# A decoder layer on one core: weighted values of two chunks at a time, sums built in place, a new order

## The chip, the cores and the metric

One core of a Trainium2 chip runs the whole layer. The metric is the device time of one execution in microseconds (us). The engines are PE (matrix multiplications), DVE (VectorE), ACT (ScalarE), POOL (GpSimd) and SP, whose queue issues nearly all transfers. The time before is 3048.16 us, the median of three runs (3047.43 to 3048.79).

## The reference

The inputs are x and a context, both 64 x 128 x 512 in float32. One layer does this, where `_layernorm` has no weights:

```python
x = _layernorm(x + _L0_attn_ref(x, Wqkv, q_norm_w, k_norm_w, Wo))   # 16 heads of 32; RMS norm of q and k, rotary, causal
x = _layernorm(x + _L0_xattn_ref(x, ctx, ctx))                      # 8 heads
x = _layernorm(x + _L0_ffn_ref(x, weight))                          # both sides quantized to fp8 in blocks of 128

# cross attention: channels and positions change roles; q, k, v are (b, 128, 512)
qh, kh, vh = q.reshape(b*8, 16, 512), k.reshape(b*8, 16, 512), v.reshape(b*8, 16, 512)
qk = einsum('bdm,bdn->bmn', qh, kh) / sqrt(16)      # 512 x 512 scores for each head
ret = einsum('bmn,bcn->bcm', softmax(qk), vh)
```

Cross attention is the largest part: for each of the 64 batches and 8 heads it takes a softmax over 512 x 512 scores with a sum over only 16 rows.

## The kernel before

The program goes over 64 batches of 128 rows of x. Three stages of different batches are at work at the same time, and a planner in the kernel writes their operations out in one fixed order for each engine.

**Self attention** (`self_attention`). x is transposed, multiplied by the three thirds of `wqkv` (`project`, L322), normalized and rotated (DVE L435, POOL L441), transposed again (L328) to `hT`. Scores come in two halves, each of eight small matmuls with 32 rows (L462, row tiles of the array). For each of four groups of heads follow the mask addition and the negated maximum on DVE (L472, L475), four exponentials on ACT (L480), the reciprocal (L483), a scaling on POOL (L484), a transpose and a copy to `pT`. `outs` (L497) multiplies by v in column tiles of the array, 32 columns each; `wo` (L322), the sum with x (L508) and a layer norm give `x1`.

**Cross attention.** Half a batch, four heads, is a step s. Its j-th part, with j from 0 to 7, is half of a chunk of 128 of the 512 positions: chunk c = j // 2, and two of the four heads. `split` writes q and k as three bfloat16 parts (ACT L515 and L517, POOL L516 and L518) to DRAM; `stack` reads them back with 96 rows (L550 to the tiles `ks` and `qs`, three of each). `maxima` multiplies the stacks (L569, two matmuls into the one buffer mx) and reduces (DVE L572); after eight of them the negated maxima are split in three (L579 to L582), transposed (L586) and sent as three more rows into `qs` (L589). `scores` multiplies again with 99 rows (L604, the one buffer sc), and one exponential on ACT (L607) makes half of a tile `e`. `values` (L618) multiplies a chunk of e by v in four column tiles, summed over four chunks in the one bank av, and is called for every second j:

```python
if j % 2:
    values(j // 8, j % 8 // 2, av)
```

`gather` copies av out and sends it to `ac` (values) and to DRAM (sums); `cross_norm` gets the reciprocals (L643) by way of DRAM into a tile of their own, rb (L645), multiplies (POOL L647), adds x1 (DVE L649) and normalizes to x2.

**The last stage** (`ffn`). `quantize` (L370 to L388) scales x2 by blocks (POOL L374), rounds it to fp8's steps (DVE L377, L379, POOL L381, L382) and transposes it; four matmuls (L664), a scaled product each (DVE L669) into `ft`, a sum each into `h` (POOL L671), a layer norm and the transfer out. A layer norm is L353 to L360, with `rsqrt` (L341 to L347) inside; L347 is a product of 128 single numbers.

**Order.** `Plan.op` takes an engine, a cost in us, what is read and written, and a due time; `Plan.emit` places the operations one after another by these costs, hands out PSUM banks, and charges `TURN` where PE goes from one tiling (whole array, rows, columns) to another. The table `DUE` gives each operation of a batch its due time. The instructions are emitted in the order of placing, and each engine takes its own in that order. Four pools of banks exist: sc and mx with two banks each, av with one, t with three single ones, which everything else shares.

Of the kernel before, what the change touches and what calls it, by code (L numbers as in the profile page):

```python
# [38 lines left out]
    -0.477, 6.406, 1.108, 8.738, -3.388, -1.975, 8.446, -3.211, 10.046, 7.308, 7.14, 6.348, 8.835, 8.498,  # L39
    0.443, 6.255, 8.093, 0.86, -0.351, 5.636, 7.136, 7.206, 8.857, 1.225, 8.516, 5.911, -2.993, 7.459, 8.982,  # L40
    6.702, 8.584, -5.195, 1.613, 9.25, -1.205, 8.309, 8.351, 8.7, -4.37, 6.314, 5.681, -1.329, 2.961, 0.446,
    4.994, 7.225, 7.441, 9.169, -4.195, -1.969, 6.862, 8.415, 6.701, 5.583, 6.848, -2.311, 5.936, 0.669,
    -4.336, -3.225, -0.65, 7.359, 5.273, 5.221, 6.697, 1.056, -0.699, 10.521, 7.725, 1.786, 9.317, -0.281,
    7.711, 9.842, 9.061, 1.577, 8.221, 8.006, 7.879, 8.309, -3.567, 8.595, -1.665, 7.728, 9.366, -2.72, 8.659,
    7.918, 8.136, 1.226, 7.377, 8.801, -1.9, -3.235, 7.155, 2.459, 8.078, -0.111, 7.922, -2.283, 5.744, 8.589,
    8.639, 8.798, 8.023, 8.345, -2.381, 6.687, -3.336, 7.068, 9.022, 8.525, 7.703, -3.294, 7.204, 7.939,
    6.409, 8.724, 7.655, 6.335, -1.792, 9.28, 6.159, 8.745, 9.751, 6.105, 6.091, 9.536, -2.089, -2.232, 9.199,
    0.309, 6.288, 7.752, -2.402, 7.063, 8.465, 7.427, 8.775, 8.582, 6.962, 6.325, 8.669, -0.787, -1.292,
    0.453, 0.296, 8.463, 7.71, 7.588, 7.733, 0.379, 6.155, 7.154, 4.889, 7.773, -0.595, 7.767, 9.666, -1.092,
    6.191, 6.563, 6.653, 9.013, 8.943, 0.439, -2.316, 7.671, 0.863, 7.589, 6.814, 9.034, 7.913, 8.909, 0.355,  # L50
    6.804, 8.655, -2.295, 8.48, 8.501, 6.94, 8.017, 6.906, 7.026, 8.43, -1.393, 6.234, 7.098, 1.585, 8.045,
    8.533, 0.468, 7.066, 8.861, 0.714, 8.882, 6.175, -1.35, 6.235, 7.375, 6.217, 8.925, 8.641, -1.356, 0.11,
    7.185, 9.58, 7.556, -0.724, 6.008, 0.98, 6.563, 0.096, -0.199, 6.617, 4.512, 7.397, 6.433, 1.976, 0.624,
    8.166, 0.903, 8.672, 6.633, 8.659, 7.036, 7.95, 5.571, 1.956, 8.387, 7.208, 1.108, 8.445, 5.939, 7.611,
    9.168, 10.789, 9.282, 9.545, 7.415, 7.227, 1.509, 9.523, 0.675, 8.502, 1.884, 5.826, 8.269, 5.729, 9.384,
    0.745, 8.88, 8.088, 6.299, 9.017, 6.601, 5.232,
]
NK, NX, NE, NT = 3, 4, 2, 1
# [18 lines left out]
class Plan:  # L77
# [7 lines left out]
    TURN = 0.14  # L85
# [5 lines left out]
    def op(self, engine, cost, emit, r=(), w=(), b=None, due=0.0, late=0.0, mode=0):  # L91
# [24 lines left out]
        if b is not None:  # L116
            i = self.count[b] = self.count.get(b, -1) + 1
            due = b + (DUE[i] if i < len(DUE) else due)
        self.ops.append((engine, cost, emit, due, late, banks, sorted(deps), (b, i), mode))

    def emit(self):
# [14 lines left out]
        for _ in ops:  # L136
# [4 lines left out]
            for e in ENGINES:  # L141
                mine = None
                for n in cand[e]:
                    if at[n] > limit and e != "SP":
                        continue
                    t = max(est[n], free[e] + self.TURN * (e == "PE" and ops[n][8] != turned))
                    want = {}
                    for k in ops[n][5]:
                        if k.slot is None:
                            want[k.pool] = want.get(k.pool, 0) + 1  # L150
                    open_ = {p: sorted(s[1] for s in self.pools[p] if s[2] is None) for p in want}
                    if any(len(open_[p]) < m for p, m in want.items()):
# [35 lines left out]
def decoder_kernel(  # L188
# [24 lines left out]
    nc.sync.dma_start(out=cst, in_=consts)  # L213
# [11 lines left out]
    nc.scalar.copy(ident_h, ident)  # L225
# [11 lines left out]
    r_h = ring("h", 2, [P, D])  # L237
# [16 lines left out]
    r_rb = ring("rb", 1, [P, D])  # L254
# [3 lines left out]
    r_ft = ring("ft", 2, [P, D])  # L258
# [8 lines left out]

    banks = {
        "sc": [psp.tile([P, 2, D], F32, name="sc")],
        "mx": [psp.tile([P, 2, D], F32, name="mx")],  # L270
        "av": [psp.tile([P, D], F32, name="av")],
        "t": [psp.tile([P, D], F32, name=f"ps{i}") for i in range(3)],
    }

# [63 lines left out]
    def rsqrt(v, ky, s, col, pr):  # L338
# [4 lines left out]
        op("DVE", 0.07, lambda: nc.vector.scalar_tensor_tensor(t, r, v, r, ALU.mult, ALU.mult),  # L343
# [3 lines left out]
        op("DVE", 0.07, lambda: nc.vector.tensor_tensor(lv, r, t, ALU.mult), [ky + "r", ky + "t"], [ky + "l"], pr)  # L347
        return lv, ky + "l"

    def layernorm(h, kh, y, key, pr):  # L350
        s, k = small("ln")
        st, mv, ve = s[:, 0:6], s[:, 8:10], s[:, 10:11]
        op("DVE", 0.6, lambda: nc.vector.bn_stats(st, h), [kh], [k + "st"], pr)  # L353
# [4 lines left out]
        op("DVE", 0.08, lambda: nc.vector.scalar_tensor_tensor(nb, mv[:, 0:1], -1.0, r, ALU.mult, ALU.mult),  # L358
           [k + "mv", kr], [k + "nb"], pr)
        op("ACT", 0.5, lambda: nc.scalar.activation(y, h, AF.Identity, bias=nb, scale=r),  # L360
           [kh, k + "nb", kr], [key], pr)

    def quantize(src, key, pr):
# [4 lines left out]
        am, sc, rc = s[:, 0:NC], s[:, 8 : 8 + NC], s[:, 16 : 16 + NC]  # L368
        y, e, xq = r_qy[0], r_qe[0], r_xq[0]
# [4 lines left out]
        op("POOL", 0.97, lambda: nc.gpsimd.tensor_tensor(  # L374
# [6 lines left out]
        op("POOL", 1.2, lambda: nc.gpsimd.tensor_tensor(y, y, e, ALU.add), ["qy", "qe"], ["qy"], pr)  # L381
        op("POOL", 1.2, lambda: nc.gpsimd.tensor_tensor(xq, y, e, ALU.subtract), ["qy", "qe"], ["xq"], pr)  # L382
# [9 lines left out]
    def ffn_weights(o):  # L392

        wt, key = r_h[o % 2], f"h{o % 2}"
# [10 lines left out]
    def self_attention(b):  # L405
        at = lambda f: (b, f - 2.1)
        i2 = b % 2
        x_t, kx = r_x[i2], f"x{i2}"
        op("SP", 0.4, lambda: nc.sync.dma_start(out=x_t, in_=x[b]), [], [kx], at(-0.3), 5.0)
        xT, kxT = r_xT[i2], f"xT{i2}"  # L410
        tp = Bank("t", kxT)
# [3 lines left out]
        def project(j, pr, *then):  # L415
            ps = Bank("t", *then)
# [4 lines left out]
        for j in range(2):  # L421
# [7 lines left out]
            op("ACT", 0.7, lambda ps=ps, t1=t1, ss=ss: nc.scalar.activation(t1, ps.ap, AF.Square, accum_out=ss),  # L429
# [13 lines left out]
            tp = Bank("t", f"hT{j}{i2}")  # L443
# [10 lines left out]
        for r0 in (0, 2):  # L454
            pr = at(0.35 + 0.1 * r0)
            two = [Bank("t", f"pr{(4 * b + r0 + n) % 3}") for n in range(2)]
# [8 lines left out]
            for n in range(2):  # L465
# [16 lines left out]
                op("ACT", 1.55, exps, [k], [kp, k + "su"], pr)  # L482
# [3 lines left out]
                tp = Bank("t", f"{kpT}{r}")  # L486
# [3 lines left out]
        o_ps = Bank("t", "oT")  # L490
# [12 lines left out]
        a_ps = Bank("t", "h0")  # L503
        pr = at(0.87)
        matmuls(a_ps, pr, [(oT[:, c, :], wo[:, c, :]) for c in range(NC)], ["oT"])
        h, kh = r_h[0], "h0"
        pr = at(0.95)
        op("DVE", 0.6, lambda: nc.vector.tensor_tensor(h, a_ps.ap, x_t, ALU.add), [a_ps, kx], [kh], pr)  # L508
        layernorm(h, kh, r_x1[b % NX], f"x1{b % NX}", pr)

    def split(u, b, src, key, pr):
# [3 lines left out]
        op("ACT", 0.48, lambda: nc.scalar.copy(sp[:, 0, :], src), [key], [f"sp0{n}"], pr)  # L515
        op("POOL", 1.1, lambda: nc.gpsimd.tensor_tensor(rt, src, sp[:, 0, :], ALU.subtract), [key, f"sp0{n}"], [f"rt{n}"], pr)  # L516
        op("ACT", 0.48, lambda: nc.scalar.copy(sp[:, 1, :], rt), [f"rt{n}"], [f"sp1{n}"], pr)  # L517
# [39 lines left out]
    def maxima(j):  # L557
# [21 lines left out]
        op("DVE", 0.08, lambda: nc.vector.tensor_copy(ns[:, 0, :], x), kx, [f"ns{m}0"], pr)  # L579
# [30 lines left out]
    def values(s, c, av):  # L610
        b, g = divmod(s, 2)
        n = (4 * s + c) % NE
        e, va = r_e[n], r_va[b % 2]

        def go():
            for i in range(4):
                h = 4 * g + i
                nc.tensor.matmul(  # L618
                    av.ap[32 * i : 32 * i + 32, :], lhsT=va[:, c, 32 * h : 32 * h + 32], rhs=e[:, i, :],
                    start=(c == 0), stop=(c == NC - 1))  # L620
        op("PE", 0.83, go, [f"e{n}0", f"e{n}1", f"va{b % 2}"], [av], (b, g / 2 + (2 * c + 2) / 16), mode=COLS)
# [14 lines left out]
    def cross_norm(b):  # L636
        pr = (b, 1.15)
        n = b % 2
        x1, x2, ac, rs, rb = r_x1[b % NX], r_x2[b % 2], r_ac[n], r_rs[n], r_rb[0]
# [9 lines left out]
        op("DVE", 0.6, lambda: nc.vector.tensor_tensor(h, ac, x1, ALU.add),  # L649
           [f"ac{n}0", f"ac{n}1", f"x1{b % NX}"], [kh], pr)  # L650
        layernorm(h, kh, x2, f"x2{b % 2}", pr)

    def ffn(b):
        pr = (b, 1.35)
        x2, kx2 = r_x2[b % 2], f"x2{b % 2}"
        tp, half, sc, ks = quantize(x2, kx2, pr)
# [4 lines left out]
        h, kh = r_h[1], "h1"  # L661
        for c in range(NC):
            f_ps = Bank("t", f"ft{c % 2}")
# [4 lines left out]
            ft, kt = r_ft[c % 2], f"ft{c % 2}"  # L668
            op("DVE", 0.65, lambda f_ps=f_ps, ft=ft, c=c: nc.vector.scalar_tensor_tensor(  # L669
                ft, f_ps.ap, sc[:, c : c + 1], ws[:, c, :], ALU.mult, ALU.mult), [f_ps, ks, "ws"], [kt], pr)  # L670
            op("POOL", 1.2, lambda ft=ft, c=c: nc.gpsimd.tensor_tensor(h, h if c else x2, ft, ALU.add),  # L671
               [kt] if c else [kt, kx2], [kh], pr)
        pr = (b, 1.7)
        layernorm(h, kh, y, ky, pr)
# [13 lines left out]
    for j in range(-LEAD, 16 * B):  # L688
# [11 lines left out]
        if j % 2:  # L700
# [51 lines left out]
```

## Time and profile before

| | |
|---|---|
| median of 3 runs | 3048.16 us (3047.43 to 3048.79) |
| profiled execution | 3049.07 us, its span 3047.3 us |
| granted PE clock, mean | 0.983 |
| first scores (L604) start | 116.7 us |
| last scores start | 2999.1 us |
| from one batch to the next, steady | 45.14 us |
| mean of one L572 / L607 / L671 | 1221 / 1021 / 1269 ns |
| DMA, share of 16 engines | 27.6% for the queue that SP and the others issue to |

A window's row gives its length and each engine's busy time in it, then the granted clock (1.00 is full), the share of the DMA engines and GB/s. A timeline's row gives start, duration, engine, source line, operation, result and operands, their shapes and how many instructions were merged; a bracket holds the idle time before it and who ended it. PE's durations overlap those of the next instruction, so the cost of a step is read from one start to the next. A group's row ends with the sum and mean of its busy time and the idle time before it.

### The profile page before, as it was taken

What the parts mean: (1) busy time and instruction counts of PE and PEld (TensorE: products, weight loads), DVE (VectorE), ACT (ScalarE), POOL (GpSimd) and SP (SyncE); (2) the same over time, 40 slices, a digit from 0 to 9 for tenths busy, and PEclk for the clock granted to TensorE, in tenths of its full rate; (3) what the DMA queues carried; (4) which work ended last, traced back from release to release, by engine and by line L of the source; (5) the groups of instructions that cost most, each with busy time, mean ns of one, the idle gap of its engine ahead of it and who ended that gap; (6) DMA issues with size and microseconds to landing.
All of it is one profiled execution on the core that took longest, in us unless ns stands there. A gap on an engine that the chain in (4) does not pass through costs nothing.

```text
span 3047.3 us, 51833 instructions
## 1 busy us (share of the span) xinstructions
PE 2906.7 (95%) x17040; PEld 1307.0 (43%) x17040; DVE 2632.5 (86%) x5211; ACT 2296.3 (75%) x5382; POOL 1400.1 (46%) x1309
## 2 busy tenths in 40 slices
PE   7799999999999999999999999999999999999973
PEld 3334444444444444444444444444444444444420
DVE  3668899899899899889989989989989988988974
ACT  4467877777777787787787787777778778778763
POOL 3324444454445445444445445444444544444433
PEclk8899999999999999999999999999999999999996
DMA  3422322322222223232232232222222222223220
GB/s 114 61 83 79 89 80 82 89 82 84 84 84 85 83 83 85 85 86 81 82 89 81 80 89 82 83 86 84 84 82 87 83 85 86 81 82 89 75 65 25
DMA packets 162845, 249.97 MB, mean 82 GB/s; under 512 B 45328, under 2 KB 94608, under 8 KB 162448
## 3 DMA queue, kind: packets, MB, share of 16 engines
q1 hardware_dynamic: 161472, 242.47, 27.6%
q10 hardware_dynamic: 1104, 4.19, 0.4%
q8 instruction: 135, 2.21, 0.3%
q14 instruction: 134, 1.10, 0.1%
HBM read 159.01 MB, written 69.21 MB: 75 GB/s over the span
## 4 chain that ended last, share of the span: by engine, by line
PE 52%; DVE 26%; ACT 7%; issue 5%; DMA 5%; POOL 4%; SPq 1%; POOLq 0%; ACTq 0%; DVEq 0%
PE ps L322 17%; DVE nm L572 12%; PE mx L569 9%; PE av L618 8%; PE sc L604 8%; DVE ft L669 5%; PE ps L328 4%; DMA ks<-d_k 4%; POOL pr L484 3%; DVE pr L472 3%; PE ps L462 2%; ACT e L607 2%; DVE s_ln L347 2%; ACT hT L336 2%; PE ps L497 2%
## 5 line engine op out<-in xcount | busy, mean ns | idle before, releaser
L572 DVE TENSOR_REDUCE nm<-mx 128x2 f32<-128x1024 f32 x1024 | 1250.4, 1221 | 210.0 <-PE mx L569 198.2
L607 ACT ACTIVATE e<-sc 128x1024 f32<-128x1024 f32 x1024 | 1045.7, 1021 | 510.8 <-PE sc L604 508.9
L322 PE MATMUL ps<-wqkv,xT 128*128 128x512 f32 x1536 | 761.6, 598 | 1.4 <-ACT xT L336 0.7
L569 PE MATMUL mx<-ks,qs 96*128 96x512 bf16 x2048 | 615.5, 381 | 35.6 <-DVE nm L572 14.0
L604 PE MATMUL sc<-qs,ks 99*128 99x512 bf16 x2048 | 613.8, 380 | 9.0 <-ACT e L607 8.8
L484 POOL TENSOR_TENSOR pr<-pr,s_max 128x512 f32<-128x512 f32 x256 | 266.1, 1040 | 734.8 <-DVE s_max L483 408.1
L618 PE MATMUL av<-e,va 128*32 128x512 f32 x4096 | 540.3, 605 | 2.7 <-ACT e L607 2.4
L480 ACT ACTIVATE pr<-pr,s_max 128x128 f32<-128x128 f32 x1024 | 395.3, 389 | 6.8 <-DVE s_max L475 6.8
L569 PEld LDWEIGHTS <-qs 96*128 96x128 bf16 x2048 | 176.5, 97 | 512.8 <-issue 451.9
L322 PEld LDWEIGHTS ps<-wqkv,xT 128*128 128x128 f32 x1536 | 281.7, 191 | 183.3 <-issue 97.9
L604 PEld LDWEIGHTS <-ks 99*128 99x128 bf16 x2048 | 184.1, 98 | 333.6 <-issue 187.0
L441 POOL TENSOR_TENSOR rot<-t,t 128x256 f32<-128x256 f32 x256 | 184.3, 740 | 284.5 <-DVE t L435 271.3
L671 POOL TENSOR_TENSOR h<-h,ft 128x512 f32<-128x512 f32 x192 | 243.7, 1269 | 58.6 <-DVE ft L669 48.5
L322 PE MATMUL ps<-wo,oT 128*128 128x512 f32 x512 | 243.7, 598 | 0.0
L669 DVE SCALAR_TENSOR_TENSOR ft<-ps,s_fp,ws 128x512 f32<-128x512 f32 x256 | 179.8, 743 | 22.6 <-PE ps L664 19.9
L472 DVE TENSOR_TENSOR pr<-ps,cst 128x512 f32<-128x512 f32 x256 | 164.6, 684 | 39.4 <-PE ps L462 39.3
L336 ACT COPY pT<-ps 128x512 f32<-128x512 f32 x256 | 144.0, 587 | 71.5 <-PE ps L328 71.0
L480 ACT ACTIVATION_READ_ACCUMULATOR pr<-pr,s_max 128x1 f32 x1024 | 193.2, 189 | 0.0
L518 POOL TENSOR_TENSOR sp<-rt,sp 128x512 bf16<-128x512 f32 x128 | 148.2, 1158 | 94.2 <-ACT sp L517 94.2
L328 PE MATMUL ps<-cst,pr 128*128 128x128 f32 x1024 | 149.3, 278 | 30.3 <-POOL pr L484 30.3
L328 PEld LDWEIGHTS ps<-cst,pr 128*128 128x128 f32 x1024 | 115.8, 142 | 133.7 <-POOL pr L484 101.1
L618 PEld LDWEIGHTS av<-e,va 128*32 128x32 f32 x4096 | 94.2, 108 | 181.2 <-issue 145.5
(85 smaller groups left out, 3736.2 us busy)
## 6 DMA issues: line engine op xcount, KB each, us to landing
d_k<-sp SPq DMA_DIRECT2D x192, 128.0 KB
ks<-d_k SPq DMA_DIRECT2D x128, 192.0 KB
d_q<-sp SPq DMA_DIRECT2D x192, 128.0 KB
qs<-d_q SPq DMA_DIRECT2D x128, 192.0 KB
x<-in_x_dram SPq DMA_DIRECT2D x64, 256.0 KB
cx<-in_ctx_dram SPq DMA_DIRECT2D x64, 256.0 KB
ks<-d_k SPq DMA_DIRECT2D x128, 128.0 KB
qs<-d_q SPq DMA_DIRECT2D x128, 128.0 KB
```

Of the source, the lines that this page charges most:

```text
L322: op("PE", 0.86, lambda k=k, a=lhsT, b=rhs: nc.tensor.matmul(bank.ap, lhsT=a, rhs=b, start=(k == 0), stop=(k == len(parts) - 1)), r, [bank ...
L328: nc.tensor.transpose(bank.ap[:, c * P : (c + 1) * P], src[:, c * P : (c + 1) * P], ident)
L472: op("DVE", 0.6, lambda pc=pc, bk=two[n]: nc.vector.tensor_tensor(pc, bk.ap.rearrange("p (c k) -> p c k", k=P), mask[:, None, :].to_broadc ...
L480: nc.scalar.activation(pc[:, c, :], pc[:, c, :], AF.Exp, bias=nm[:, c : c + 1], accum_out=su[:, c : c + 1])
L484: op("POOL", 0.97, lambda pc=pc, rs=rs: nc.gpsimd.tensor_tensor(pc, pc, rs[:, :, None].to_broadcast([P, NC, P]), ALU.mult), [k + "rs"], [k ...
L569: nc.tensor.matmul(M.ap[:, k, :], lhsT=qs[0:NSP, i, c * P : (c + 1) * P], rhs=ks[0:NSP, i, :], start=True, stop=True)
L572: op("DVE", 1.14, lambda: nc.vector.tensor_reduce(nm[:, 2 * p : 2 * p + 2, c], M.ap, AX.X, ALU.max, negate=True), [M], [f"nm{m}{c}{p}"], pr)
L604: nc.tensor.matmul(A.ap[:, k, :], lhsT=ks[0 : NSP + 3, i, c * P : (c + 1) * P], rhs=qs[0 : NSP + 3, i, :], start=True, stop=True)
L607: op("ACT", 0.92, lambda: nc.scalar.activation(e[:, 2 * p : 2 * p + 2, :], A.ap, AF.Exp, scale=scale), [A], [f"e{m}{p}"], pr)
L618: nc.tensor.matmul(av.ap[32 * i : 32 * i + 32, :], lhsT=va[:, c, 32 * h : 32 * h + 32], rhs=e[:, i, :], start=(c == 0), stop=(c == NC - 1))
L669: op("DVE", 0.65, lambda f_ps=f_ps, ft=ft, c=c: nc.vector.scalar_tensor_tensor(ft, f_ps.ap, sc[:, c : c + 1], ws[:, c, :], ALU.mult, ALU.m ...
L671: op("POOL", 1.2, lambda ft=ft, c=c: nc.gpsimd.tensor_tensor(h, h if c else x2, ft, ALU.add), [kt] if c else [kt, kx2], [kh], pr)
```

## The change

- `values` takes two chunks at a time (every fourth j), eight matmuls in column tiles of the array in a row; there are three tiles e instead of two.
- Sums stand in place: the residual of self attention in x's tile, that of cross attention in `ac`, that of the last stage in y. The tiles h, rb and ft are gone; the reciprocals and the scaled products use `qe` and `qy`, tiles of `quantize`.
- The first batch's self attention takes its banks from sc (as two single ones) and av instead of t.
- x of batch 0 is the first transfer, and `wqkv` comes in three thirds of its columns instead of four of its rows.
- In the last batch the POOL operations of `quantize`, `cross_norm` and `ffn` are done by DVE.
- The planner has other costs, charges 0.1 for a turn, adds 0.05 to what PE finishes, and may place an operation early if it holds a bank already; `DUE` is another table.

```diff
-NK, NX, NE, NT = 3, 4, 2, 1
+NK, NX, NE, NT = 3, 4, 3, 1
...
-    TURN = 0.14
+    TURN = 0.1
...
+        late += 0.05 * (engine == "PE")
...
-                    if at[n] > limit and e != "SP":
+                    if at[n] > limit and e != "SP" and all(k.slot is None for k in ops[n][5]):
...
+        "first": [sc[:, 0, :], sc[:, 1, :], av],
...
+    nc.sync.dma_start(out=r_x[0], in_=x[0])
+    nc.sync.dma_start(out=cst, in_=consts)
+    for j in range(3):
+        cols = slice(j * D, (j + 1) * D)
+        nc.scalar.dma_start(out=wqkv[:, :, cols], in_=w_qkv[:, cols].rearrange("(c p) n -> p c n", p=P))
...
-        op("POOL", 0.97, lambda: nc.gpsimd.tensor_tensor(
+        op(eng, 0.6 if last else 0.97, lambda: en.tensor_tensor(
             y, s3, rc[:, :, None].to_broadcast([P, NC, P]), ALU.mult), [key, k + "rc"], ["qy"], pr)
...
+        pool = "t" if b else "first"
...
-                op("ACT", 1.55, exps, [k], [kp, k + "su"], pr)
+                op("ACT", 1.46, exps, [k], [kp, k + "su"], pr)
...
-        op("DVE", 0.6, lambda: nc.vector.tensor_tensor(h, a_ps.ap, x_t, ALU.add), [a_ps, kx], [kh], pr)
-        layernorm(h, kh, r_x1[b % NX], f"x1{b % NX}", pr)
+        op("DVE", 0.6, lambda: nc.vector.tensor_tensor(x_t, a_ps.ap, x_t, ALU.add), [a_ps], [kx], pr)
+        layernorm(x_t, [kx], r_x1[b % NX], f"x1{b % NX}", pr)
...
     def values(s, c, av):
+
         b, g = divmod(s, 2)
-        n = (4 * s + c) % NE
-        e, va = r_e[n], r_va[b % 2]
+        ns, va = [(4 * s + k) % NE for k in (c - 1, c)], r_va[b % 2]
 
         def go():
-            for i in range(4):
-                h = 4 * g + i
-                nc.tensor.matmul(
-                    av.ap[32 * i : 32 * i + 32, :], lhsT=va[:, c, 32 * h : 32 * h + 32], rhs=e[:, i, :],
-                    start=(c == 0), stop=(c == NC - 1))
+            for k, n in zip((c - 1, c), ns):
+                for i in range(4):
+                    h = 4 * g + i
+                    nc.tensor.matmul(
+                        av.ap[32 * i : 32 * i + 32, :], lhsT=va[:, k, 32 * h : 32 * h + 32], rhs=r_e[n][:, i, :],
+                        start=(k == 0), stop=(k == NC - 1))
...
+        eng, en = ("DVE", nc.vector) if b == B - 1 else ("POOL", nc.gpsimd)
...
+        rb = flat(r_qe[0])
...
         op("SP", 0.4, lambda: nc.sync.dma_start(out=rb, in_=d_rs[n][:, None, :].to_broadcast([2 * NC, XD, D])),
-           [f"d_rs{n}"], ["rb"], pr, 5.0)
...
+           [f"d_rs{n}"], ["qe"], pr, 5.0)
...
-        op("DVE", 0.6, lambda: nc.vector.tensor_tensor(h, ac, x1, ALU.add),
-           [f"ac{n}0", f"ac{n}1", f"x1{b % NX}"], [kh], pr)
-        layernorm(h, kh, x2, f"x2{b % 2}", pr)
...
+        op("DVE", 0.6, lambda: nc.vector.tensor_tensor(ac, ac, x1, ALU.add), [f"x1{b % NX}"], ka, pr)
+        layernorm(ac, ka, x2, f"x2{b % 2}", pr)
...
-            f_ps = Bank("t", f"ft{c % 2}")
+            f_ps = Bank("t", ("qy", "qe")[c % 2])
...
-            op("POOL", 1.2, lambda ft=ft, c=c: nc.gpsimd.tensor_tensor(h, h if c else x2, ft, ALU.add),
-               [kt] if c else [kt, kx2], [kh], pr)
+            op(eng, 0.6 if b == B - 1 else 1.23, lambda ft=ft, c=c: en.tensor_tensor(y, y if c else x2, ft, ALU.add),
+               [kt] if c else [kt, kx2], [ky], pr)
...
-        if j % 2:
+        if j % 4 == 3:
             values(j // 8, j % 8 // 2, av)
```

## The prediction

> **What bounds the kernel now.** I read the busy times first, then windows of steady work, then one batch in order of time, then the groups of VectorE.
>
> ```profile
> PE 2906.7 (95%) x17040; PEld 1307.0 (43%) x17040; DVE 2632.5 (86%) x5211; ACT 2296.3 (75%) x5382; POOL 1400.1 (46%) x1309
> 1000.00:1500.00 500.00, 494.29 (x2959) 224.54 (x2957) 452.13 (x897) 395.47 (x929) 237.91 (x221) 1.00 0.29 84
> 1491.24:1536.38 45.14, 44.62 (x267) 20.20 (x266) 40.84 (x82) 35.74 (x85) 21.53 (x20) 1.00 0.28 84
> ```
>
> The first line is the page's; the others are windows (length; PE, PEld, DVE, ACT, POOL busy). PE is full, DVE is busy 40.84 of 45.14 us. The pattern repeats: a batch's transposes of x start at 1491.24 and 1536.39, and nearly every batch from the 15th on takes 45.14.
>
> Where PE's 45.14 us go is read from the starts on its timeline:
>
> ```profile
> 1505.79 0.60 PE L569 MATMUL mx<-ks,qs 96*128 96x512 bf16 x2
> 1506.79 0.66 PE L328 MATMUL ps<-cst,pr 128*128 128x128 f32 x4 [0.40 <-POOL pr L484]
> 1507.37 1.06 PE L618 MATMUL av<-e,va 128*32 128x512 f32 x8
> 1508.25 1.06 PE L497 MATMUL ps<-pT,v 128*32 128x128 f32 x32
> 1509.13 1.04 PE L618 MATMUL av<-e,va 128*32 128x512 f32 x8
> 1510.10 0.61 PE L569 MATMUL mx<-ks,qs 96*128 96x512 bf16 x2
> ...
> 1517.90 0.59 PE L569 MATMUL mx<-ks,qs 96*128 96x512 bf16 x2
> 1518.42 1.95 PE L618 MATMUL av<-e,va 128*32 128x512 f32 x16
> 1520.31 0.60 PE L604 MATMUL sc<-qs,ks 99*128 99x512 bf16 x2
> ```
>
> Start to start, a pair of mx or sc takes 0.44 us beside others of its kind (whole array). Before a column-tiled run it takes 0.52: entering costs 0.08 to 0.09. A chunk of weighted values takes 0.88 inside a run, and 0.97 to 1.00 before whole-array work: leaving costs 0.10 to 0.14. Two chunks together take 1.89. Added up over this batch, PE's stalls (0.57 before the transpose at 1506.79, 0.24 and 0.13 before mx, 0.11 of small ones) make 1.05; without them the batch would take 44.1.
>
> DVE is the second bound: mx has one buffer. Its reduction starts 0.63 after the matmuls, and the next mx starts 1.27 after the reduction (1504.32 below; from 1531.43 to 1532.70 elsewhere). And DVE is held up beside POOL:
>
> ```profile
> 1503.08 0.18 DVE L483 RECIPROCAL s_max<-s_max 128x4 f32<-128x4 f32 x1
> ...
> 1503.34 1.04 POOL L484 TENSOR_TENSOR pr<-pr,s_max 128x512 f32<-128x512 f32 x1 [5.69 <-DVE s_max L483]
> ...
> 1503.59 0.81 DVE L347 TENSOR_TENSOR s_ln<-s_ln 128x1 f32<-128x1 f32 x1
> ...
> 1504.32 1.21 DVE L572 TENSOR_REDUCE nm<-mx 128x2 f32<-128x1024 f32 x1
> ```
>
> L347 multiplies 128 numbers and needs 0.16 alone; here it ends with POOL's L484 (1504.38), which its own DVE neighbour L483 had released 0.26 earlier. The groups say how common that is:
>
> ```profile
> L347 DVE TENSOR_TENSOR s_ln<-s_ln 128x1 f32<-128x1 f32 x192 | 125.9, 656 | 6.6
> L649 DVE TENSOR_TENSOR h<-ac,x 128x512 f32<-128x512 f32 x64 | 67.5, 1055 | 2.3 <-ACT y L360 2.3
> L472 DVE TENSOR_TENSOR pr<-ps,cst 128x512 f32<-128x512 f32 x256 | 164.6, 684 | 39.4 <-PE ps L462 39.3
> ```
>
> With one input in PSUM (L472) 0.68; with both in SBUF (L649) 1.06. Three L347 of 0.50 and one L649 of 0.38 too much are 1.9 us of DVE a batch. Today they hardly reach PE: mx's waits for DVE are 0.24.
>
> **What the change moves on PE.** The matmuls are the same in number and kind. The built orders have 1035 changes of tiling before and 892 after. In a steady batch it is eight tiled runs against seven: before, one pair of chunks already stood together and another two chunks stood around the outputs of self attention (L497); after, there are four pairs and L497 alone, and two runs of L462 as before. One run fewer is one entry and one exit, 0.09 + 0.14 = 0.23, less a flip of 0.03 inside two more pairs: 0.2 us a batch. PE without stalls: 44.1 - 0.2 = 43.9.
>
> **Where DVE then stands.** I followed the new order from the first masked scores of a batch (end of the row-tiled L462, called 0) to the third mx after it; durations are start to start in the batch above. PE: mx 0.44, sc 0.44, transpose 0.44, projection 0.86, sc 0.44, two projections 1.72 (second mx at 4.33); mx 0.44, projection 0.86, transpose 0.44, entry 0.09, two chunks with exit 1.88, transpose 0.44 (third mx at 8.48); mx and sc 0.87, entry and L497 with exit 1.07: fourth mx at 10.42. DVE: two mask additions and two maxima done by 2.57 (1499.32 to 1501.88 in the old trace, the same group), reduction to 3.70; it waits for the exponentials' sums until 4.14 (e to pT to four exponentials: 0.63 + 0.44 + 0.92 + 0.48 + 1.67), then small ones and L435 to 5.29; reduction to 6.42; reciprocal, L435, L649, L353 and seven small ones, 2.66, to 9.08; reduction from 9.11, so the fourth mx may start at 10.38. PE wants it at 10.42. The room is 0.04 us, with no wait beside POOL counted.
>
> Such waits must come there. The reciprocal at 4.14 releases POOL's 1.04 us L484 0.25 later, and L347 stands 0.29 behind that reciprocal: up to 1.0, or nothing if it slips ahead. The next reciprocal releases the next L484 while the addition of cross attention (L649's successor) stands 0.74 behind: 0.5 to 0.9. Then POOL has the two turns (1.42) and L516 (1.16) in a row, and another L347 falls among them: 0.2 to 0.9. On PE this is 0.35 to 1.5 us at the fourth mx. Two smaller waits precede it: a projection behind the second mask addition (0.2), and the values behind the last e, which stands behind eight exponentials on ACT (0.2). Two mx further on, L347 meets POOL's L518: 0 to 0.55 (room 0.24, block 0.8). Two mx in the dense stretch stand 1.74 apart where 1.90 is needed: 0.15. Last, the maxima's split L579 to L582 now stands right behind the third scaled product L669, whose POOL sum (1.27) starts 0.06 before L580; the transpose of the split waits on PE: 0 to 0.67. L580's own row shows no such wait (174 to 177 ns in 128 executions), but it never stood beside POOL; L347, the nearest row with both inputs in SBUF, says 0.67. I take half.
>
> Sum of new stalls: 0.9 at the least, 3.3 at the most; I take 2.1, between ends far apart nearer to the row of L347, which shows the wait in two of its three places in this batch (0.16, 0.81, 1.12). Batch: 43.9 + 2.1 = 46.0 (44.8 to 47.2), against 45.14: +0.86 (-0.35 to +2.05). About 58 batches run at this pace (the first scores of batch 3 start at 263, those of batch 61 at 2886): **+50 us (-20 to +119)**.
>
> The Trainium skill (SBUF — State Buffer, section Who interferes with whom) says that a VectorE instruction with two SBUF inputs and a GpSimd instruction that reads SBUF exclude each other, the later one blocking fully. By this rule L580 would be blocked like L347, where its own row shows nothing; L347's 0.81 agrees with it. It speaks against this change, and by it the batch would be 0.33 us longer than I take it.
>
> **Start and end.** In the old start the first x1 ends late:
>
> ```profile
> 39.82 0.48 PE L462 MATMUL ps<-hT,hT 32*128 32x128 f32 x2
> 51.89 2.81 PE L462 MATMUL ps<-hT,hT 32*128 32x128 f32 x16
> 54.63 6.58 PE L322 MATMUL ps<-wo,oT 128*128 128x512 f32 x8
> ```
>
> The second half of batch 0's scores (39.82) moves right behind the first transposed probabilities (34.30): -5 us. Batch 1's scores (51.89) leave the place before the output projection: -3. Another 9 us stall (PE idle to 157.66, behind DMAs) may go or stay. Start: -12 (-25 to 0). Other banks for batch 0 and weights by columns only serve this. At the end, batch 63's sums move to DVE: quantizing -0.36 and twice -0.59 (1.04 and 1.27 against 0.68), the products and sums 5.0 (four of 0.65, four of 0.6) against 6.1 (3034.91 to 3041.0): -2.6. But the reciprocals now land in qe, which batch 62's sums still read, so that transfer (0.64 to issue, 2 to 5 to land) and then the addition stand behind them, where 3.4 us lay before (3019.57 to 3022.96): +0 to +4. I take 0 in sum. In steady work that transfer makes SP wait for the last POOL sum; queued behind it are the next ks and qs, first read some 20 us later: nothing. Sums in place, the third e, and x held longer cost nothing while that holds; if a late x showed, it would be a 7 us landing. Altered costs in the planner act through the order alone.
>
> **Forecast and rivals.** Profiled execution: 3049.07 (span 3047.3 and 1.8 around it), 0.9 above the median 3048.16, from which I count: 3048 + 50 - 12 = 3086, rounded to 3085. Forecast, 63%: slower, DVE's waits beside POOL reach PE.
> Rival 1, 31%: faster. The small L347 slips ahead of POOL, the split too, and PE's own waits give DVE the room: 44.8 a batch, 3048 - 20 - 12 = 3016; without any wait 43.9, 3048 - 72 - 12 = 2964. For it: PE's busy 99% leaves few waits today. Against it: 0.04 us of room. It decides below 45.35 a batch, where -12 from the start is used up.
> Rival 2, 6%: fewer turns and new stalls cancel, 45.25 to 45.45, within 0.2%, about what a measurement here can tell from no change.
> Rival 3, inside the 63% (12%): all blocks at their worst, 47.2, 3155.
> Alone, the forecast's range is 3056 to 3145; with rival 1 down to 3003 and the top at 3140, some 2 in 10 are left out.
>
> **What would show it.** Right: a steady period above 45.4; mx's waits for DVE nm well above 14 us in sum; L347 and the cross-attention addition no shorter in the mean; PE waiting between L497 and the next mx; first sc before 110. Wrong: a period under 45.1 with mx waiting under 0.3 us a batch, or waits for DMA (qs, ks, rb) on PE, which I priced at nothing.

## The result and the profile after

The changed kernel takes 3137.28 us, the median of four runs (3132.57 to 3138.52), where the kernel before took 3048.47 beside it (3047.43 to 3054.70): a ratio of 1.0284, 95% interval 1.0266 to 1.0302. It is slower, by 89 us and not by the 37 forecast.

Line numbers have moved: L322 is now L327, L328 is L333, L342 to L347 are L347 to L352, L358 is L363, L435 and L441 are L442 and L448, L462 is L469, L472 is L479, L484 is L491, L497 is L504, L516 and L518 are L522 and L524, L569 and L572 are L575 and L578, L579 to L582 are L585 to L588, L586 is L592, L604 is L610, L618 is L625, L649 is L658, L669 and L671 are L678 and L680.

The page's busy times of the profile after:

```profile
PE 2937.8 (94%) x17040; PEld 1321.8 (42%) x17040; DVE 2755.7 (88%) x5219; ACT 2314.2 (74%) x5382; POOL 1401.9 (45%) x1301
```

Windows of the same profile, 500 us and one batch (length; PE, PEld, DVE, ACT, POOL busy; clock, DMA share, GB/s):

```profile
1000.00:1500.00 500.00, 484.17 (x2840) 218.89 (x2838) 458.89 (x862) 387.30 (x908) 235.53 (x217) 1.00 0.28 81
2317.17:2363.72 46.55, 45.17 (x267) 20.45 (x266) 42.88 (x82) 35.91 (x84) 21.74 (x21) 1.00 0.27 81
```

The same work, VectorE busy for 42.88 us instead of 40.84 though it has no more to do, and TensorE idle for 1.4 us a batch instead of 0.5. From the first scores of batch 3 to the last scores the profile takes 2823.3 us (264.4 to 3087.8), before 2735.8: 87.5 of the 88.8 us by which the spans differ. Before batch 3 lie 1.2 of it (264.4 against 263.2), behind the last scores 0.15 (48.36 against 48.21).

In one batch, the end of the first row-tiled L469 at 2331.09 (the 0 of the prediction's walk) and the four maxima on TensorE's timeline:

```profile
2331.09 0.60 PE L575 MATMUL mx<-ks,qs 96*128 96x512 bf16 x2
...
2335.64 0.60 PE L575 MATMUL mx<-ks,qs 96*128 96x512 bf16 x2
...
2339.81 0.60 PE L575 MATMUL mx<-ks,qs 96*128 96x512 bf16 x2
2340.25 0.60 PE L610 MATMUL sc<-qs,ks 99*128 99x512 bf16 x2
2340.78 1.17 PE L504 MATMUL ps<-pT,v 128*32 128x128 f32 x32
2342.94 0.59 PE L575 MATMUL mx<-ks,qs 96*128 96x512 bf16 x2 [1.00 <-DVE nm L578]
```

The fourth mx comes at +11.85 instead of +10.42. L504 to mx takes 2.16 us where 1.14 would do (a_ptr, below, takes 1.14 there). VectorE and POOL in the same stretch of the timeline:

```profile
2338.75 1.87 POOL L448 TENSOR_TENSOR rot<-t,t 128x256 f32<-128x256 f32 x2
...
2339.98 0.65 DVE L348 SCALAR_TENSOR_TENSOR s_rms<-s_rms 128x1 f32<-128x1 f32 x1
...
2340.57 1.16 POOL L522 TENSOR_TENSOR rt<-cx,sp 128x512 f32<-128x512 f32 x1
...
2340.85 0.90 DVE L352 TENSOR_TENSOR s_rms<-s_rms 128x1 f32<-128x1 f32 x1
2341.68 1.21 DVE L578 TENSOR_REDUCE nm<-mx 128x2 f32<-128x1024 f32 x1
```

Two products of 128 numbers take 0.65 and 0.90 us. Each ends as POOL's instruction ends (2340.62 and 2341.73), and the reduction that frees mx waits behind the second. The split, earlier in the batch:

```profile
2326.74 0.17 DVE L586 TENSOR_TENSOR nm<-nm,ns 128x16 f32<-128x16 f32 x1
...
2326.76 1.28 POOL L680 TENSOR_TENSOR y<-y,qy 128x512 f32<-128x512 f32 x1 [0.66 <-DVE ns L585]
...
2326.95 1.13 DVE L587 CAST ns<-nm 128x16 bf16<-128x16 f32 x1
...
2328.11 0.17 DVE L588 TENSOR_TENSOR ns<-nm,ns 128x16 bf16<-128x16 f32 x1
...
2328.34 0.24 PE L592 MATMUL ps<-ident_h,ns 128*48 128x128 bf16 x1 [0.38 <-DVE ns L588]
```

The subtraction L586 started 0.02 ahead of POOL's sum and took 0.17; the cast behind it was held until the sum's end. In the groups of VectorE (count, sum, mean ns, idle before):

```profile
L352 DVE TENSOR_TENSOR s_rms<-s_rms 128x1 f32<-128x1 f32 x128 | 63.8, 498 | 2.3
...
L587 DVE CAST ns<-nm 128x16 bf16<-128x16 f32 x128 | 78.5, 613 | 4.3
...
L658 DVE TENSOR_TENSOR ac<-ac,x 128x512 f32<-128x512 f32 x64 | 69.7, 1089 | 5.4 <-POOL ac L656 5.3
```

The first two in the kernel before:

```profile
L347 DVE TENSOR_TENSOR s_rms<-s_rms 128x1 f32<-128x1 f32 x128 | 22.2, 173 | 2.3
...
L581 DVE CAST ns<-nm 128x16 bf16<-128x16 f32 x128 | 23.3, 182 | 2.3
```

The costliest waits of TensorE from 300 to 2900 us (sum, times, longest):

```profile
PE mx L575 <- DVE nm L578: 59.3, 79, 1.0
...
PE ps L592 <- DVE ns L588: 21.3, 56, 0.4
```

### The profile page after: what moved, and what is told of

Same layout as the page of the kernel before. It is cut to its first block, busy times and chain, and to the rows that moved or that the text cites. A ratio compares the mean times of both kernels' runs of the same rounds, so it can differ in the third digit from the quotient of the medians.

```text
span 3136.1 us, 51390 instructions
## 1 busy us (share of the span) xinstructions
PE 2937.8 (94%) x17040; PEld 1321.8 (42%) x17040; DVE 2755.7 (88%) x5219; ACT 2314.2 (74%) x5382; POOL 1401.9 (45%) x1301
## 4 chain that ended last, share of the span: by engine, by line
PE 57%; DVE 30%; issue 5%; ACT 5%; DMA 1%; POOL 1%; SPq 0%; POOLq 0%; ACTq 0%; DVEq 0%
PE ps L327 19%; PE mx L575 12%; PE sc L610 9%; DVE nm L578 9%; PE av L625 8%; PE ps L469 4%; DVE t L442 3%; ACT pr L487 3%; DVE pr L479 2%; DVE ns L587 2%; DVE ac L658 2%; DVE s_rms L352 2%; PE ps L333 2%; DVE qy L678 1%; DVE s_rms L348 1%
## 5 line engine op out<-in xcount | busy, mean ns | idle before, releaser
L578 DVE TENSOR_REDUCE nm<-mx 128x2 f32<-128x1024 f32 x1024 | 1247.9, 1219 | 155.2 <-PE mx L575 141.2
L613 ACT ACTIVATE e<-sc 128x1024 f32<-128x1024 f32 x1024 | 1046.2, 1022 | 428.0 <-PE sc L610 425.5
L327 PE MATMUL ps<-wqkv,xT 128*128 128x512 f32 x1512 | 768.8, 611 | 0.2 <-ACT xT L341 0.2
L575 PE MATMUL mx<-ks,qs 96*128 96x512 bf16 x2048 | 617.4, 383 | 88.5 <-DVE nm L578 77.9
L610 PE MATMUL sc<-qs,ks 99*128 99x512 bf16 x2048 | 616.8, 382 | 13.5 <-ACT e L613 13.3
L625 PE MATMUL av<-e,va 128*32 128x512 f32 x4096 | 501.3, 608 | 0.0
L491 POOL TENSOR_TENSOR pr<-pr,s_max 128x512 f32<-128x512 f32 x256 | 267.7, 1046 | 304.7 <-DVE s_rms L350 226.8
L575 PEld LDWEIGHTS <-qs 96*128 96x128 bf16 x2048 | 184.2, 98 | 479.1 <-issue 427.3
L610 PEld LDWEIGHTS <-ks 99*128 99x128 bf16 x2048 | 189.7, 98 | 399.9 <-issue 237.3
L327 PEld LDWEIGHTS ps<-wqkv,xT 128*128 128x128 f32 x1512 | 268.2, 190 | 160.3 <-issue 97.0
L522 POOL TENSOR_TENSOR rt<-x,sp 128x512 f32<-128x512 f32 x64 | 74.1, 1158 | 568.1 <-ACT sp L521 568.1
L448 POOL TENSOR_TENSOR rot<-t,t 128x256 f32<-128x256 f32 x256 | 207.4, 830 | 225.1 <-DVE t L442 207.6
L479 DVE TENSOR_TENSOR pr<-ps,cst 128x512 f32<-128x512 f32 x252 | 167.5, 686 | 85.4 <-PE ps L469 85.3
L327 PE MATMUL ps<-wo,oT 128*128 128x512 f32 x504 | 238.4, 594 | 0.0
L625 PEld LDWEIGHTS av<-e,va 128*32 128x32 f32 x4096 | 108.3, 110 | 253.0 <-issue 251.5
L680 POOL TENSOR_TENSOR y<-y,qe 128x512 f32<-128x512 f32 x126 | 160.8, 1276 | 107.1 <-DVE qe L678 106.5
L680 POOL TENSOR_TENSOR y<-x,qy 128x512 f32<-128x512 f32 x63 | 80.1, 1272 | 278.9 <-DVE qy L678 278.9
L482 DVE TENSOR_REDUCE s_max<-pr 128x4 f32<-128x512 f32 x256 | 168.2, 678 | 0.1
L333 PE MATMUL ps<-cst,pr 128*128 128x128 f32 x1008 | 159.3, 281 | 8.4 <-POOL pr L491 7.5
L333 PEld LDWEIGHTS ps<-cst,pr 128*128 128x128 f32 x1008 | 115.6, 142 | 118.2 <-POOL pr L491 100.1
```

The source lines that it names most:

```text
L327: op("PE", 0.86, lambda k=k, a=lhsT, b=rhs: nc.tensor.matmul(bank.ap, lhsT=a, rhs=b, start=(k == 0), stop=(k == len(parts) - 1)), r, [bank ...
L333: nc.tensor.transpose(bank.ap[:, c * P : (c + 1) * P], src[:, c * P : (c + 1) * P], ident)
L448: nc.gpsimd.tensor_tensor(vr[:, :, t, :], v1[:, :, t, :], v2[:, :, 1 - t, :], ALU.add)
L479: op("DVE", 0.6, lambda pc=pc, bk=two[n]: nc.vector.tensor_tensor(pc, bk.ap.rearrange("p (c k) -> p c k", k=P), mask[:, None, :].to_broadc ...
L491: op("POOL", 0.97, lambda pc=pc, rs=rs: nc.gpsimd.tensor_tensor(pc, pc, rs[:, :, None].to_broadcast([P, NC, P]), ALU.mult), [k + "rs"], [k ...
L575: nc.tensor.matmul(M.ap[:, k, :], lhsT=qs[0:NSP, i, c * P : (c + 1) * P], rhs=ks[0:NSP, i, :], start=True, stop=True)
```

## Experiments

Theory: VectorE's small instructions are held up beside POOL, and that reaches TensorE through mx's one buffer and the split. Rivals: the new order loses time whatever POOL does; the pairs of values or the sums in place cost time themselves. Kernels named a_ are the changed one, b_ the one before, each with one edit. "A batch" is the median time from a start of scores to the same one a batch later (1600 starts, from the 200th on). Of the changed kernel's batches some take 46.55 and some 46.72, in the mean from batch 3 to 61 46.62. Each ran beside runs of the kernel before on its own chip, whose medians were 3049.7 (with a_ptr, a_cast and the thin ones), 3056.6 (a_single, a_start0, a_ptr_ws, b_ptr), 3058.1 (b_pair, b_pair_ptr) and 3052.6 us (b_ptr_ends, a_ptr_cast); so ratios are compared, not times.

| kernel | a batch, us | median, us | ratio to before (95%) |
|---|---|---|---|
| before | 45.14 | 3048.5 | 1 |
| after | 46.56 | 3137.3 | 1.0284 (1.0266 to 1.0302) |
| a_ptr | 45.34 | 3062.7 | 1.0042 (1.0027 to 1.0057) |
| a_cast | 46.34 | 3123.4 | 1.0242 (1.0225 to 1.0259) |
| a_ptr_cast | 45.13 | 3045.4 | 0.9981 (0.9967 to 0.9995) |
| a_thin / b_thin | 44.78 / 44.38 | 3012.9 / 2989.3 | one run each |
| a_single | 48.21 | 3240.8 | 1.0604 (1.0588 to 1.0620) |
| b_pair / b_pair_ptr | 47.50 / 46.92 | 3205.6 / 3170.0 | 1.0477 (1.0460 to 1.0495) / 1.0365 (1.0348 to 1.0382) |
| a_start0 | 46.55 | 3141.4 | 1.0276 (1.0260 to 1.0291) |
| a_ptr_ws | 45.34 | 3063.6 | 1.0022 (1.0012 to 1.0032) |
| b_ptr | 44.53 | 3018.8 | 0.9878 (0.9863 to 0.9892) |
| b_ptr_ends | 44.53 | 3010.2 | 0.9862 (0.9845 to 0.9879) |

**The form of the smallest instructions (a_ptr).**

```diff
-nc.vector.scalar_tensor_tensor(t, r, v, r, ALU.mult, ALU.mult)
+nc.vector.tensor_scalar(t, r, v, r, ALU.mult, ALU.mult)
...
-nc.vector.tensor_tensor(lv, r, t, ALU.mult)
+nc.vector.tensor_scalar(lv, r, t, None, ALU.mult)
...
-nc.vector.scalar_tensor_tensor(nb, mv[:, 0:1], -1.0, r, ALU.mult, ALU.mult)
+nc.vector.tensor_scalar(nb, mv[:, 0:1], r, -1.0, ALU.mult, ALU.mult)
```

> The changed kernel, its order untouched, with the three smallest vector instructions (L348, L352, L363, 128x1) written with their factors as per-partition scalars, so that each reads one tensor from SBUF and not two. Theory (held up): 128x1 instructions that read two SBUF tensors wait out a POOL instruction, those that read one (L350, L360: 147 ns on average) don't. L348, L352 and L363 fall from 238-498 ns to below 200 on average, the fourth maxima (L575) of a batch come 0.6 to 1.2 us earlier, a batch takes 45.4 to 46.0 instead of 46.6, the time is 3065 to 3100. Rival (the order alone): these instructions are late because of what stands ahead of them in the order, whatever their form: they may shorten, but the batch stays within 0.2 of 46.6 and the time at 3125 to 3140.

1.22 us a batch are gone, of the 1.42 lost; by the ratios it is 85% of the loss (0.0242 of 0.0284), in the same order with POOL's work untouched. The same place of the batch on a_ptr's timeline:

```profile
2420.00 1.86 POOL L448 TENSOR_TENSOR rot<-t,t 128x256 f32<-128x256 f32 x2
...
2421.23 0.26 DVE L348 TENSOR_SCALAR s_rms<-s_rms 128x1 f32<-128x1 f32 x1
...
2421.71 0.21 DVE L352 TENSOR_SCALAR s_rms<-s_rms 128x1 f32<-128x1 f32 x1
...
2421.84 1.22 DVE L578 TENSOR_REDUCE nm<-mx 128x2 f32<-128x1024 f32 x1
...
2423.13 0.60 PE L575 MATMUL mx<-ks,qs 96*128 96x512 bf16 x2
```

L348 runs through in the midst of L448, 0.26 where it took 0.65. The first mx of this batch stands at 2412.31, so the fourth is at +10.82, 1.03 earlier. The waits for nm at L575, 59.3 us from 300 to 2900, are no longer among TensorE's waits there (a one-time 0.4 at L575 is left). The order alone is not the reason; it chose what stands beside what.

**The split (a_cast).**

```diff
-nc.vector.tensor_copy(ns[:, 1, :], x)
+nc.vector.tensor_reduce(ns[:, 1, :], x[:, :, None], AX.X, ALU.max)
```

(and so for `ns[:, 0, :]`)

> The changed kernel, its order untouched, with the two casts of the split (L585, L587, 128x16 to bf16) done as a reduction over an axis of length one, the form of L578, which no POOL instruction lengthened. Theory (held up): L587 falls from 613 ns on average to below 250, TensorE's wait for the split at L592 loses some 0.45 us once a batch, the batch goes to 46.1 to 46.3 and the time to 3108 to 3122. Rival: the last step L588 (two SBUF tensors) is held up in its place, and the time stays at 3130 to 3140.

The result lies between the two expectations. The groups of VectorE in a_cast:

```profile
L588 DVE TENSOR_TENSOR ns<-nm,ns 128x16 bf16<-128x16 f32 x128 | 67.5, 527 | 2.3
...
L587 DVE TENSOR_REDUCE ns<-nm 128x16 bf16<-128x16 f32 x128 | 21.7, 170 | 4.3
```

The cast as a reduction is not held (613 to 170), but the last subtraction now is (179 to 527), since it comes while POOL's sum still runs (in one batch it takes from 2452.51 to 2453.44, and the sum ends at 2453.41). TensorE's wait at L592 falls from 21.3 us to 9.6, and from batch 3 to the last scores 14.5 us are gained, 0.24 a batch.

**POOL's work cut down (a_thin, b_thin).** Each POOL tensor operation of the plan went through this:

```diff
+    def thin(en, o, a, b, f):
+        if en is nc.gpsimd:
+            o, a, b = (v[..., 0:8] for v in (o, a, b))
+        en.tensor_tensor(o, a, b, f)
```

> The changed kernel, its order untouched, with each POOL tensor operation done on 8 of the columns of its innermost axis only (what is left out of the computation: the rest of these products and sums). Theory (held up): with POOL nearly idle nothing is held up; the sum of VectorE's work falls by 2 us a batch, the batch to 44.1 to 44.6 and the time to 2995 to 3020. Rival (the order, the pairs or the sums in place lose the time by themselves): the batch stays above 46.0 and the time above 3105.

> The kernel before with its POOL tensor operations cut in the same way, as the control. Theory (held up): its batch goes from 45.14 to 44.1-44.5 and the time to 2985 to 3010, so that the two kernels without POOL's work lie within 25 us of each other instead of 89. Rival: this one gains as much as the changed kernel does or more, and the distance between the two stays above 60 us.

One batch of a_thin, then of b_thin, in the view of windows:

```profile
2366.25:2411.03 44.78, 44.77 (x268) 20.21 (x267) 38.88 (x81) 35.85 (x85) 5.49 (x20) 1.00 0.31 85
```

```profile
2347.86:2392.24 44.38, 44.35 (x267) 20.36 (x266) 39.05 (x82) 35.51 (x86) 5.27 (x20) 1.00 0.30 85
```

With POOL at 5 us a batch both kernels leave TensorE no idle time, and the changed one is 24 us behind instead of 89. POOL's presence costs the changed kernel 1.78 us a batch and the one before 0.76; the cut also brings POOL's results earlier, so this bounds the hold-ups from above. But 0.40 us a batch stays, where I had expected both kernels alike and had forecast a gain of 0.2 for the pairs. Added up by starts on TensorE's timeline over one batch, entries and exits of the tiled forms cost 1.75 in a_thin and 1.89 in b_thin. Starts elsewhere that are 0.03 to 0.19 late make 0.91 in a_thin (eleven) and 0.32 in b_thin (three). So fewer visits to the tiled form save 0.14, and 0.59 comes back in late starts, in all 0.45 of loss by these rows against the 0.40 measured. Three of a_thin's are inside projections (0.10 each), five at transposes of pr (0.03 to 0.17). What delays each of these is not settled.

**The pairs undone in the new order (a_single).** The first half of each pair is issued ahead of the TensorE group that stands before it:

```diff
+            if two:
+                i = max(i for i, (f, _) in enumerate(seq) if f == "PE")
+                seq[i:i] = [("PE", two[0])]
```

> The changed kernel with the pairs alone undone: of each pair of chunks (L625) the first one's four matmuls are issued ahead of the TensorE group that stands before the pair, all else in the planned order; 512 more changes of tiling, eight a batch. Theory (a visit to the tiled form costs 0.09 in and 0.14 out): four visits more are 0.92 us a batch, of which the one ahead of the fourth maxima may vanish in the wait there; a batch takes 47.1 to 47.5, the time is 3165 to 3195. Rival (pairs cost time, since the scores behind them wait for 1.7 us of values instead of 0.85): the time falls to 3105-3130.

The sign was that of the theory and the size too small, and the rival was wrong: 1.65 us a batch more, not 0.5 to 0.9. The outputs of self attention and the fourth mx in one batch (L513 and L584 of this file):

```profile
2560.41 0.42 PE L513 MATMUL ps<-pT,v 128*32 128x128 f32 x6
2561.10 1.06 PE L513 MATMUL ps<-pT,v 128*32 128x128 f32 x26 [0.27 <-ACT pT L350]
2562.65 0.59 PE L584 MATMUL mx<-ks,qs 96*128 96x512 bf16 x2 [0.49 <-DVE nm L587]
```

On the timeline four more entries and exits (0.10 and 0.14 each) make 0.97. The rest are new waits: the outputs lose 0.53 within themselves (0.27 of it stands as a wait for ACT's pT, 14.8 us in sum from 300 to 2900), and scores and maxima behind two of the halves are 0.2 and 0.4 late. The wait at the fourth mx took up 0.45. In this order the pairs are worth more than I gave them.

**The pairs alone, in the old order (b_pair, b_pair_ptr).** The planned order of the kernel before is kept; each even chunk waits for the odd one:

```diff
+            elif c % 2 == 0:
+                held = go
+            else:
+                seq += [held, go]
```

> The kernel before with its own planned order kept, and the weighted values of two chunks made one after the other: each even chunk's four matmuls wait until the odd chunk's turn, with three sets of exponentials; the room comes from sums built in the tiles ac, y, xT, qy and qe in place of their own. Changes of tiling fall from 1035 to 773. Theory (the pairs pay and the new order is what loses): 4.1 changes fewer a batch at 0.09 in and 0.14 out are 0.47 us, a batch takes 44.6 to 44.9, the time is 3015 to 3035. Rival 1 (1.7 us of values in a row keep scores and maxima waiting): 45.1 to 45.6 a batch, 3040 to 3070. Rival 2 (the sums in place bring new waits): waits on VectorE or POOL at the layer norms and 3050 or more.

> b_pair with the three 128x1 vector instructions in the form with per-partition scalars, as in b_ptr. Theory: both gains add, 44.69 less 0.47 is 44.2 a batch; the time is 2980 to 3000, below both kernels. Rival (they are the same slack, taken twice): 3010 to 3020, as b_ptr.

My theories fell here, b_pair's by some 170 us, and rival 1 was right in kind (scores and maxima wait) and too small. Changes of tiling are 773, fewer than in either kernel, and a batch takes 47.50. TensorE and VectorE on b_pair's timeline:

```profile
2507.29 0.59 PE L578 MATMUL mx<-ks,qs 96*128 96x512 bf16 x2
2507.72 0.59 PE L613 MATMUL sc<-qs,ks 99*128 99x512 bf16 x2
...
2507.91 1.23 DVE L581 TENSOR_REDUCE nm<-mx 128x2 f32<-128x1024 f32 x1 [0.68 <-PE mx L578]
...
2509.20 0.59 PE L578 MATMUL mx<-ks,qs 96*128 96x512 bf16 x2 [0.88 <-DVE nm L581]
...
2528.65 1.08 PE L506 MATMUL ps<-pT,v 128*32 128x128 f32 x32 [0.67 <-ACT pT L345]
...
2549.62 0.59 PE L578 MATMUL mx<-ks,qs 96*128 96x512 bf16 x2 [1.05 <-DVE nm L581]
```

(L578, L613, L581 and L506 are the mx, sc, nm and outputs of self attention of this file.) Before, an even chunk's values stood between that sc and that mx, and their 1.0 us was the time in which VectorE emptied mx. Taken away, mx follows at once and waits: 0.88 here, 1.05 at the second such place, and the outputs wait 0.67 for ACT's pT. These make 2.60, two visits fewer give back 0.47; 2.13 of the 2.36 measured. At the first place VectorE had been idle for 0.68 just before, waiting for mx itself. So pairs need another order, and "the pairs" and "the order" have no separate prices: undoing the pairs costs 1.65 us in the new order, and making them costs 2.4 in the old one. Of rival 2, waits from the sums in place, there is no sign: no wait of TensorE at or behind a layer norm is among the costly ones. The sums were not tried without the pairs. b_pair_ptr takes off 0.58 and stays slower than before.

**The start undone (a_start0).**

```diff
-        pool = "t" if b else "first"
+        pool = "t"
...
-    nc.sync.dma_start(out=r_x[0], in_=x[0])
...
-        nc.scalar.dma_start(out=wqkv[:, :, cols], in_=w_qkv[:, cols].rearrange("(c p) n -> p c n", p=P))
+        nc.scalar.dma_start(out=wqkv[:, c, :], in_=w_qkv[c * P : (c + 1) * P, :])
```

> The changed kernel with the start alone undone: the first input loaded by the plan, the weights in four row pieces, the first self attention in the three banks t as in the kernel before. Theory (the start's 6 us are lost again at the wait for the queries of the second half, 4.9 us at 175.6-180.5, and the half clock behind it): first scores at 116 to 118, but the third batch at most 4 us later than in the changed kernel; time 3133 to 3142. Rival (the start does its work and the order loses it elsewhere): first scores and the third batch both 6 to 12 us later, time 3143 to 3150.

First scores at 111.8 instead of 110.7 (I had said 116 to 118), batch 3 at 266.9 instead of 264.4, the ratio the same. The loads and banks bring 1 to 3 us; the rest, from 116.7 to 111.8, lies in what a_start0 keeps, mostly the order (not tried apart).

**The late queries (a_ptr_ws).**

```diff
-               [f"d_ws{o}" for o in range(NC)], ["ws"], -1.0, 2.5)
+               [f"d_ws{o}" for o in range(NC)], ["ws"], 0.3, 2.5)
```

> The kernel a_ptr with the broadcast of the weight scales (L408, 128x2048) issued three transfers later, behind the last piece of the queries (L556) and the two stores of the first sums. Theory (the 4.9 us wait of the maxima L575 at 175.6 is for that piece, which lies behind the broadcast): the wait goes, the clock doesn't fall to 0.50 for the 11 us after it, and the third batch starts 6 to 11 us earlier; time 3051 to 3057 where a_ptr took 3062.7. Rival (the queries come late for the split of the first batch's own reasons): 3060 to 3065.

Windows of the changed kernel, of 4 us each, show what is at stake (the column before the DMA share is the granted clock):

```profile
172.00:176.00 4.00, 2.92 (x24) 0.93 (x23) 3.13 (x7) 0.92 (x3) 2.74 (x3) 1.00 0.91 269
176.00:180.00 4.00, 0.00 (x0) 0.00 (x0) 0.00 (x0) 1.11 (x2) 1.98 (x2) 0.88 0.20 53
180.00:184.00 4.00, 3.51 (x9) 1.85 (x10) 1.23 (x1) 0.59 (x1) 0.00 (x0) 0.50 0.04 8
...
188.00:192.00 4.00, 4.00 (x9) 1.76 (x8) 3.02 (x7) 3.38 (x12) 0.00 (x0) 0.50 0.00 0
192.00:196.00 4.00, 4.00 (x15) 1.86 (x14) 2.35 (x5) 2.44 (x10) 2.03 (x2) 0.91 0.22 47
```

TensorE waits 4.9 us, then works at half clock until 192. With the broadcast moved, the wait in a_ptr_ws is 3.6 us instead of a_ptr's 5.3, the clock from 165 to 193 us 0.94 instead of 0.79 in the mean, and batch 3 starts at 261.7 instead of 266.5. That is 4.8 us, below the 6 to 11 expected. The wait is only 1.7 of it and the rest goes with the clock, which the move need not have changed: in a_cast, whose start is as in the changed kernel, TensorE waits 4.1 us, the half clock ends at 182.5, and batch 3 starts at 260.2 instead of 264.4. The ratio moved from 1.0042 to 1.0022, with intervals that overlap. So the broadcast was at most a part of the wait, and what its move is worth in the whole time stays open.

**The small forms in the kernel before (b_ptr).** The edit of a_ptr.

> The kernel before, its order untouched, with the three smallest vector instructions (L343, L347, L358) in the form with per-partition scalars. Theory (held up): L347 falls from 656 to some 210 ns on the layer norms, 1.3 us of VectorE a batch, but TensorE waits for VectorE little in this order: its batch goes from 45.2 to 44.8-45.1 and the time to 3022 to 3042. Rival (none of it reaches TensorE): 3045 to 3052.

Better than expected: 0.61 us a batch. L347 on the layer norms had cost the old order too, spread over its many small waits. The wait at the transpose of pr from 300 to 2900 us, in the kernel before and then in b_ptr:

```profile
PE ps L328 <- POOL pr L484: 21.9, 57, 0.4
```

```profile
PE ps L328 <- POOL pr L484: 1.0, 1, 1.0
```

So even a wait that names POOL can hang on VectorE: L483, which starts POOL's scaling, stood behind the held instructions. That link is read from the order, not tested.

**Two more (b_ptr_ends, a_ptr_cast).** b_ptr_ends is b_ptr with the change's loads at the start and the last batch's POOL steps on VectorE; a_ptr_cast has both edits named.

> b_ptr with two parts of the change that leave the order of the batches alone: the start's loads (first input ahead of the constants, weights in three column parts) and the last batch's POOL steps on VectorE. Theory: first scores 1 to 6 us earlier than b_ptr's 114.8, the stretch from the last scores to the end 1 to 3 us shorter; in all 2 to 9 us, 3010 to 3017, ratio 0.985 to 0.987 against b_ptr's 0.988. Rival (the start is lost at the second half's queries, and the last batch's VectorE work queues where POOL's ran beside it): within 2 us of b_ptr, 3017 to 3022.

> The changed kernel with both edits, the 128x1 instructions in the form with scalars and the split's casts as reductions. Theory (the two gains lie at different places of the batch, fourth maxima and split, and add): 45.38 less 0.21 is 45.15 a batch and the time 3046 to 3056. Rival (a common slack): 3060 to 3066.

b_ptr_ends: first scores 113.6 instead of 114.8, batch 3 at 259.7 instead of 263.5, from the last scores to the end 47.0 instead of 49.3 (48.2 in the kernel before). It is the fastest kernel here that does all the work, 1.4% below before; its interval overlaps with b_ptr's. a_ptr_cast: the two gains add, 45.13. With five instructions in another form the changed kernel is 0.2% below the kernel before, but that one with the same three (b_ptr) is 1% further down.

## Why the prediction was right and wrong

**Right: the sign and its mechanism.** mx wanted at +10.42 and its bank freed late by small instructions beside POOL: the wait at L504 is 1.02 us, within 0.35 to 1.5, and a_ptr takes it away. POOL's two turns, 1.42 in the prediction's walk, took 1.87 there. The waits that I listed are, as measured in the batch above: 1.02 at the fourth mx, 0.14 behind the second mask addition (I had 0.2), nothing at the values behind the last e (0.2), about 0.15 two mx later (0 to 0.55; L348 was held for 0.47 there by L448, and L363 for 1.01 by L524, the L518 of before), 0.17 for two mx close together (0.15), 0.45 at the split (half of 0 to 0.67). Together 1.93 against the 2.1 that I took.

**Wrong: the stall-free 43.9.** The step "44.1 - 0.2 = 43.9" took the new order to lose nothing but the listed waits. 46.55 less 43.9 is 2.65, and the listed waits make 1.93. With POOL nearly idle a_thin still takes 44.78, and b_thin 44.38: visits to the tiled form did cost 0.14 less (0.2 forecast), but 0.59 of starts late by about a tenth came up elsewhere. (Two of the listed waits, 0.14 and 0.17, stand in a_thin as well, so the two lists overlap by 0.31.) Without POOL's work the new order is 0.40 a batch slower, where the step says 0.2 faster. That is the 0.6 us a batch by which 46.0 missed, and 35 of the 51 us by which the time did. What delays those starts stays open.

**Wrong: the start.** "-12 (-25 to 0)": the first scores came 6.0 us earlier, and by batch 3 it was 1.2 later. The 9 us stall that "may go or stay" came in another place as 4.9 us of waiting and 12 us of half clock. That and the missing gain are 13 us. The end, "0 in sum", is 0.15; its term of -2.6 for VectorE's sums is -2.3 in b_ptr_ends against b_ptr (46.98 and 49.28), where the reciprocals keep their own tile.

**The rivals.** Rival 1 needed L347's successor, L352, to slip ahead. At its first place it did (2335.49, 0.16 us, as POOL's L491 started); at the second L348 before it was held, and then L352 itself; at the third L352 was not held, but L348 and L363 around it were (0.47 and 1.01). What would show it: the waits of mx for nm are 77.9 us over the whole profile where 14.0 were (right), L658 is no shorter (1089 ns, before 1055: right), L352 is longer than L347 was in self attention (498 ns, before 173) but shorter in the layer norms (238, before 656), and first scores before 110 missed by 0.7.

**The split and the rule.** I priced L580, with two inputs in SBUF. It was not held (L586, 0.17); the cast behind it was, with one input. The Trainium skill (SBUF — State Buffer, Who interferes with whom) lists casts and operations with scalars among those that can take VectorE's second pair of ports, and says that `tensor_reduce` never contends on this chip; L587's 613 ns as a cast and 170 as a reduction agree. The prediction went by the sentence on two inputs alone.

## What to carry to other kernels

When TensorE feeds another engine through one buffer, the unrelated work between two uses is what hides that engine; moving it to save a tenth at each change of form can expose a whole microsecond (b_pair). Compare the spacing of those uses before counting what is saved. And look at the mean time of the smallest VectorE instructions: where 128 numbers take 0.5 us, another form of the same product may be worth more than a new order (b_ptr, 1.2%).

## What the runs showed of the hardware

- A product of 128x1 written with both factors as per-partition scalars is not held beside POOL (0.26 us in the midst of L448), the form with two or three SBUF tensors is (0.65 at the same place). One input is not enough for safety: the scaling L378 (128x4, a constant factor) takes 712 ns in the changed kernel and 160 in a_thin, while L350 (128x1, constants) takes 140 to 151 in both.
- After a wait of 4.9 us the clock stayed at 0.50 for 12 us with TensorE busy (180.5 to 192.7); in a_cast, after a wait of 4.1 us at the same place that ended 1 us earlier, for 3 us (179.5 to 182.5). The Trainium skill (TensorE: Matmul & The Clock Gate, Part 1) gives about 3.4 us until full clock, which a_cast's row matches and the changed kernel's does not. What makes the difference is open.
